# Cross attention in f32: product 7 of y ahead of product 5, T1 of e by ScalarE and transfers, in batches 2 to 5

## The chip, the cores and the metric

The kernel runs on one core of a Trainium2 chip. The metric is the device time of one execution in microseconds (us), as the median of several runs. TensorE multiplies matrices into PSUM, VectorE (DVE in the profile) and ScalarE (ACT) do the element work, GpSimd (POOL) reduces over partitions and issues the transfers that add to their destination, and SyncE (SP) issues the plain transfers. All transfers share 16 DMA engines.

## The reference

Eight batches; x1 and x2 are 512 x 1024 each, all f32. D is 64.

```
q = einsum('bcn,dc->bnd', x1, Wq) + bq
k = einsum('bcn,dc->bdn', x2, Wk) + bk[:, None]
v = einsum('bcn,dc->bdn', x2, Wv) + bv[:, None]
attn = softmax(einsum('bnd,bdm->bnm', q, k), axis=2)
out = einsum('bcm,bnm->bcn', v, attn) + x1
```

## The kernel before

The value projection is moved behind the attention: for each batch the kernel computes y = x2 times the unnormalized exponentials e (transposed), divides by the sums of e, and multiplies by Wv ("o" = Wv y). Both large products are done with seven block products instead of eight (Strassen's scheme in Winograd's form): the operands are cut into 2 x 2 blocks, and sums S1 to S4 of the left operand's blocks and T1 to T4 of the right one's are formed first. In y's first level the left blocks a["11"] to a["22"] are tiles of x2, and the right blocks are the halves of e. T1 = e12 - e11, T2 = T1 + e22, T3 = e22 + e12, T4 = e21 - T2. Most of the seven products are themselves done with seven smaller ones: left_stream (L543) forms the inner sums of a left operand, right_stream (L556) those of a right one, both as a few VectorE instructions that a caller interleaves with others (weave, L517). multiply_seeded (L764) then runs the inner steps 1, 7, 6, 2, 5, 4, 3 on TensorE. After most steps ScalarE copies the running sum ("chain", or "third") out of PSUM into the next quarter of the result, and the steps that follow add to these quarters. The function complete, returned by it, adds the copy v of step 7 to the result's second half on VectorE.

The program is one long list, written out by hand (manual schedule). Each engine runs its own instructions in the order in which the Python code issues them, and waits where an operand is not there yet or a tile's slot is still in use. A tile's slot is named by its tag; with one buffer per tag the next tile of that tag may be written only when every reader of the last one is done, transfers included.

period(s, n, nn, nnn) at L1154 is one batch's turn: s is the batch, n, nn and nnn are the next three. Batches 2 to 5 are marked s.six (L128). In such a period TensorE runs: products 1, 2 and 6 of y; the first half of n's scores (scores_0, L1180); nn's queries; products 5, 7 and 3 of y; the second half of n's scores; nn's keys; product 4 of y interleaved with product 1 of o; then products 6, 2, 5 with 7 with 3, and 4 of o.

What the change touches:

- sum_e and right_sums (L355, L394) form T1 to T4 on VectorE in two halves. In the kernel before, T1 of the next batch is formed at the end of the period (L1547), and T2 = T1 + e22 early in the next (L1272). T3 is formed in place of e12 by two adding transfers (sum_t3, L381).
- copy_t4 and add_t4 (L366, L375): T4 is -e21, copied by ScalarE, plus T2, added by two transfers of 512 KB on GpSimd's queue.
- copied_s4 and add_s4 (L150, L155): S4 likewise. evict_o (L949) brings a block of o out of PSUM; its function leave has x1 added by a transfer on GpSimd's queue (L983) and then sends the block out on SyncE's queue (L984). n.leave (L1568) is the list of leaves run in the next period.
- copy_7 (L901) takes product 7 out of bank "c" on ScalarE, negated, into tag u1; join_67 (L898) adds it to u6 on VectorE; evict_y "22" (L920) adds that to product 5 in bank "a".
- scores_0 also holds copy_u6, a transfer that adds u1 to u6 (L1185), add_t4, the running maxima of n's scores (folds), and the inner sums of product 7's right operand.
- shares (L330) inverts the sums of e and spreads them to all partitions through GpSimd's queue; lower (L338) subtracts the maximum; exponential (L347) is on ScalarE.
- project and queries (L186, L202): nn's queries use PSUM bank "c0"; load_x (L132) then fetches nn's x2 over the same tile, in four transfers on SyncE's queue.

Of the kernel before, what the change touches and what calls it, by code (L numbers as in the profile page):

```python
# [11 lines left out]
ALU = mybir.AluOpType  # L12
# [3 lines left out]
def kernel(  # L16
# [47 lines left out]
    nc = tc.nc  # L64
# [290 lines left out]
    def right_sums(t, k):  # L355

        x, y = {"T1": ("12", "11"), "T2": ("T1", "22"), "T3": ("22", "12")}[k]
        nc.vector.tensor_tensor(t[k], t[x], t[y], ALU.subtract if k == "T1" else ALU.add)
# [16 lines left out]
    def add_t4(s):  # L375

        t4 = s.t["T4"]
        for i in (0, 2):
            nc.gpsimd.dma_start(t4[:, i : i + 2, :], s.t["T2"][:, i : i + 2, :], accum_op=ALU.add)

# [172 lines left out]
    def inner_left(s, i, x, tag):  # L553
        weave(left_stream(s, i, x, tag))
# [599 lines left out]
    def period(s, n, nn, nnn):  # L1154
# [25 lines left out]
        def scores_0():  # L1180
            then = scores_and(n, 0, 1, "c", next_queries if nn else nothing)
            if s.six:
                copy_u6(s, 0)
                copy_u6(s, 1)
                nc.gpsimd.dma_start(s.tmp[6], s.tmp[1], accum_op=ALU.add)  # L1185
                add_t4(s)
                weave(folds(n, 0, "max", ALU.max), right_stream(s, 7, s.t["T3"], "yT1", "yT2"))
                highest(n, 0)
            elif s.b:
                sums_7 = right_stream(s, 7, s.t["T3"], "yT1", "yT2")  # L1190
# [77 lines left out]
        else:  # L1268
# [55 lines left out]
            if n:  # L1324
                weave(left_stream(s, 7, s.a["S3"], "yT4"))
            if s.six:
                weave(*sums_5)
            else:
                if s.b == 1:
                    sum_a(s, "S4")  # L1330
                    total_1(s)
            if n:
                if nn is None:
                    spread(s, 0)
                evict_q = scores_0()
                if nn:
                    spread(s, 0)
            if n is None:
                weave(right_stream(s, 7, s.t["T3"], "yT1", "yT2"), left_stream(s, 3, s.a["S4"], "aI3"))
# [25 lines left out]
            if n:  # L1365
                hooks |= {6: lambda: exponential(n, 0, 0), 4: lambda: exponential(n, 0, 1)}
            copy_7(s, 0)
            if n:
                lower(n, 0, 1)
# [12 lines left out]
            join_67(s)  # L1382
            evict_y(s, "22")
# [53 lines left out]
        if five:  # L1437
# [4 lines left out]
            sums_o7 = right_stream(s, "o7", s.y["T3"], "eT1")  # L1442
# [112 lines left out]
        if n:  # L1555
# [12 lines left out]
            n.leave = [last] if five else [leave, last]  # L1568
# [51 lines left out]
```

## Time and profile before

| | |
|---|---|
| median of 3 runs | 665.04 us (664.57 to 665.33) |
| profiled execution, its own time | 665.49 us |
| span from first to last instruction | 663.5 us |
| TensorE busy | 658.6 us (99%) |
| VectorE busy | 625.3 us (94%) |
| ScalarE busy | 379.0 us (57%) |
| GpSimd busy | 208.9 us (31%) |
| transferred | 129.05 MB, 195 GB/s on the mean |
| granted TensorE clock | 0.999 |

In the profile a row of a timeline gives start and length in us, the engine, the line of the kernel, the operation, what it writes and reads, and how many like it were merged; in brackets the idle time of the engine before it and what ended it. A row of a transfer group gives the issuing queue, the number, the size and the median time from issue to landing. The mean share of the 16 DMA engines in a stretch can exceed 1 a little, as packets overlap. Times in rows count from the span's start.

### The profile page before, as it was taken

The page shows a single profiled execution, that of the slowest core. Times are in us where ns is not written, and L with a number is a line of the kernel's source. Part 1 is how long each engine was busy: PE and PEld are TensorE (multiplying, and loading weights), DVE is VectorE, ACT ScalarE, POOL GpSimd, SP SyncE. Part 2 cuts the span into 40 slices and gives each one's busy share as a digit, 9 for nine tenths or more (in the row PEclk, how much of TensorE's full clock was granted, in tenths as well). Part 3 has the DMA queues.
Part 4 walks back from the last instruction along what each step waited for, and adds up shares of the span by engine and source line. Part 5 has one row for each costly group of instructions (what it writes and reads, how often), then busy time and mean ns, then how long its engine had stood idle before and what let it go on. Part 6 is the DMA issues. An engine that isn't in the chain of part 4 may idle for free.

```text
span 663.5 us, 8006 instructions
## 1 busy us (share of the span) xinstructions
PE 658.6 (99%) x2626; PEld 434.2 (65%) x2626; DVE 625.3 (94%) x890; ACT 379.0 (57%) x727; POOL 208.9 (31%) x179
## 2 busy tenths in 40 slices
PE   9999999999999999999999999999999999999997
PEld 5435755756658666677666686576865757666865
DVE  1999999999999999999999999999999999999997
ACT  3755457446475575665766646756567446474332
POOL 0125215631335402363034430354212640224300
PEclk9999999999999999999999999999999999999999
DMA  8687578994789759897598895987928995368614
GB/s 326 261 271 256 124 250 150 212 259 144 261 170 223 190 161 282 177 232 192 145 285 175 206 239 161 250 178 182 277 50 197 217 204 175 78 128 183 121 40 150
DMA packets 47368, 129.05 MB, mean 195 GB/s; under 512 B 5472, under 2 KB 5984, under 8 KB 47328
## 3 DMA queue, kind: packets, MB, share of 16 engines
q0 software_dynamic: 20336, 55.12, 45.8%
q1 hardware_dynamic: 26848, 73.29, 30.4%
q8 instruction: 21, 0.34, 0.2%
q14 instruction: 19, 0.16, 0.1%
q10 hardware_dynamic: 144, 0.14, 0.1%
HBM read 87.83 MB, written 16.81 MB: 158 GB/s over the span
## 4 chain that ended last, share of the span: by engine, by line
PE 94%; DVE 5%; issue 1%; ACT 0%
PE ps_yc L596 9%; PE ps_ya L596 7%; PE ps_oc L485 7%; PE ps_oa L730 6%; PE ps_s L236 6%; PE ps_ya L485 4%; PE ps_q L191 4%; PE ps_oa L485 4%; PE ps_i5chain L596 3%; PE ps_k L191 3%; PE ps_i7chain L596 3%; PE ps_i4b L881 3%; PE ps_i1chain L596 3%; PE ps_i2chain L596 3%; PE ps_i3chain L596 3%; PE ps_oc L881 2%
## 5 line engine op out<-in xcount | busy, mean ns | idle before, releaser
L340 DVE TENSOR_TENSOR e<-e,top 128x1024 f32<-128x1024 f32 x60 | 72.1, 1217 | 0.2 <-POOL top L272 0.2
L349 ACT ACTIVATE e<-e 128x1024 f32<-128x1024 f32 x60 | 62.8, 1058 | 15.9 <-DVE e L340 15.5
L272 POOL PARTITION_ALL_REDUCE top<-max x16 | 32.1, 2008 | 103.6 <-DVE max L266 44.2
L245 ACT COPY e<-ps_s 128x512 f32<-128x512 f32 x90 | 47.7, 619 | 10.2 <-PE ps_s L236 10.2
L304 POOL PARTITION_ALL_REDUCE den<-sum x10 | 33.4, 3337 | 43.2 <-DVE sum L266 38.3
L236 PE MATMUL ps_s<-q,k 64*128 64x512 f32 (+1 forms) x188 | 46.6, 598 | 0.0
L256 DVE TENSOR_TENSOR max<-max,e 128x1024 f32<-128x1024 f32 x30 | 36.5, 1218 | 0.3
L236 PEld LDWEIGHTS ps_s<-q,k 64*128 64x128 f32 x188 | 17.5, 186 | 19.9 <-issue 16.9
L916 DVE TENSOR_TENSOR y<-y,den 128x1024 f32<-128x1024 f32 x24 | 29.2, 1220 | 0.3
L787 ACT COPY ps_yc<-ps_i7chain 128x256 f32<-128x256 f32 x32 | 11.4, 357 | 30.2 <-PE ps_i7chain L596 25.6
L787 ACT COPY ps_ya<-ps_i1chain 128x256 f32<-128x256 f32 x28 | 10.0, 357 | 31.6 <-PE ps_i1chain L596 28.1
L730 PE MATMUL ps_oa<-yT,w_S 128*128 128x512 f32 x56 | 27.5, 592 | 0.0
L285 POOL PARTITION_ALL_REDUCE den<-sum x6 | 19.4, 3229 | 25.3 <-DVE sum L266 25.3
L730 PE MATMUL ps_oa<-y,w_S 128*128 128x512 f32 x56 | 26.3, 592 | 0.0
L325 POOL DMA_DIRECT2D den<-row x12 | 6.7, 561 | 60.0 <-DMA row<-few 36.6
L191 PE MATMUL ps_q<-x_in_x_dram,wqk_sb 128*64 128x512 f32 x112 | 25.6, 598 | 0.0
L485 PE MATMUL ps_oc<-yT,w 128*128 128x512 f32 x56 | 25.3, 594 | 0.1
L787 ACT COPY ps_ya<-ps_i5chain 128x256 f32<-128x256 f32 x32 | 11.5, 360 | 24.1 <-PE ps_i5chain L596 20.0
L485 PE MATMUL ps_oa<-yT,w_S 128*128 128x512 f32 x56 | 25.2, 593 | 0.0
L550 DVE TENSOR_TENSOR aI<-a 128x256 f32<-128x256 f32 x60 | 24.7, 411 | 0.0
L596 PE MATMUL ps_yc<-e,aI 128*128 128x256 f32 x92 | 23.6, 379 | 0.0
L983 POOL DMA_DIRECT2D r<-in_x_dram x14 | 18.3, 1309 | 15.9 <-ACT r L971 15.9
(358 smaller groups left out, 1861.3 us busy)
## 6 DMA issues: line engine op xcount, KB each, us to landing
x_in_x_dram<-in_x_dram SPq DMA_DIRECT2D x60, 512.0 KB, 7.5
a<-in_x2T_dram SPq DMA_DIRECT2D x32, 512.0 KB, 5.7
aS<-in_x2T_dram POOLq DMA_DIRECT2D x21, 512.0 KB, 5.7
eT<-eT POOLq DMA_DIRECT2D x16, 512.0 KB, 11.8
r<-in_x_dram POOLq DMA_DIRECT2D x14, 512.0 KB, 7.1
uo<-in_x_dram POOLq DMA_DIRECT2D x14, 512.0 KB, 8.8
out_dram<-r SPq DMA_DIRECT2D x14, 512.0 KB, 3.3
e<-e POOLq DMA_DIRECT2D x13, 512.0 KB, 7.1
```

The costliest lines, as they stand in the source:

```text
L191: nc.tensor.matmul(ps[r, :], w_sb[:, c, :], s.x[:, c, ts(h, H)], start=(c == 0), stop=(c == CT - 1),)
L236: nc.tensor.matmul(ps[g][:, n], s.k[r, ts(i, P)], s.q[r, ts(h, H)][:, n], start=True, stop=True)
L245: nc.scalar.copy(e[:, g, i, :], ps[g])
L256: nc.vector.tensor_tensor(f, e[:, :, 0, :] if i == 1 else f, e[:, :, i, :], op)
L304: nc.gpsimd.partition_all_reduce(s.den[h], s.mx[h][:, 0, :], P, ReduceOp.add)
L340: nc.vector.tensor_tensor(e, e, top, ALU.subtract)
L349: nc.scalar.activation(e, e, AF.Exp)
L485: nc.tensor.matmul(ps, left[ka][:, k, ts(j, P)], right[kb][:, k, :], start=opens and k == 0, stop=i in (2, 3, 4) and k == n_k - 1, skip_gr ...
L596: nc.tensor.matmul(ps, s.inner[i][ka][:, k, :], s.inner[i, "t"][kb][:, k, :], start=opens and k == 0, stop=z in (2, 3, 4) and k == n_k - 1 ...
L730: nc.tensor.matmul(ps, w[ka][:, k, ts(j, P)], s.y[kb][:, k, :], start=False, stop=i == 3 and k == 1, skip_group_check=True,)
L787: nc.scalar.copy(out, of)
L881: nc.tensor.matmul(ps, s.inner[i][ka][:, k, :], s.inner[i, "t"][kb][:, k, :], start=opens and k == 0, stop=z in (2, 3, 4) and k == n_k - 1 ...
```

## The change

In batches 2 to 5 (s.six):

- T1 of the next batch is no longer formed on VectorE. After the two transfers that form T3, ScalarE writes -e22 into T1 (begin_t1). In the next period VectorE forms T2 = T3 - e11 instead of T1 + e22, and two transfers add T2 to T1 (end_t1), so that T1 = T2 - e22.
- The leave of block 22 moves from the end of the period into n.leave, behind that of block 12; add_s4 and both leaves are issued behind end_t1.
- Product 7 runs before product 5. Its right sums are formed beside its left sums, ahead of the scores; product 5's inner sums are formed between the maxima in scores_0. add_t4 is issued first in scores_0, ahead of the addition of u1.
- nn's queries use a buffer of ps_s instead of bank c0.
- copy_7's two halves and join_67 move into and around product 5. Product 4's left sums are formed after evict_y "22" instead of after product 5.
- Tags: product 5's right sums use y21 for u1; product 3's left sums a12 for aI3 and its right sums eT2 for eT1; product 4's left sums aI3 for a12 and its right sums eT1 for eT2; product 7 of o's right sums eT2 for eT1.

```diff
@@ right_sums
-        x, y = {"T1": ("12", "11"), "T2": ("T1", "22"), "T3": ("22", "12")}[k]
-        nc.vector.tensor_tensor(t[k], t[x], t[y], ALU.subtract if k == "T1" else ALU.add)
+        x, y, op = {
+            "T1": ("12", "11", ALU.subtract),
+            "T2": ("T1", "22", ALU.add),
+            "T3": ("22", "12", ALU.add),
+            "T2 of T3": ("T3", "11", ALU.subtract),
+        }[k]
+        nc.vector.tensor_tensor(t[k[:2]], t[x], t[y], op)
...
+    def begin_t1(s):
+        for i in (0, 2):
+            nc.scalar.mul(s.t["T1"][:, i : i + 2, :], s.t["22"][:, i : i + 2, :], -1.0)
+
+    def end_t1(s):
+        for i in (0, 2):
+            nc.gpsimd.dma_start(
+                s.t["T1"][:, i : i + 2, :], s.t["T2"][:, i : i + 2, :], accum_op=ALU.add
+            )
@@ period
-            evict = queries(nn, "c0")
+            evict = queries(nn, None if s.six else "c0")
...
-        def scores_0():
+        def scores_0(*sums):
             then = scores_and(n, 0, 1, "c", next_queries if nn else nothing)
             if s.six:
+                add_t4(s)
                 copy_u6(s, 0)
                 copy_u6(s, 1)
                 nc.gpsimd.dma_start(s.tmp[6], s.tmp[1], accum_op=ALU.add)
-                add_t4(s)
-                weave(folds(n, 0, "max", ALU.max), right_stream(s, 7, s.t["T3"], "yT1", "yT2"))
+                weave(folds(n, 0, "max", ALU.max), *sums)
                 highest(n, 0)
...
-            sum_e(s, *(("T2",) if early else ("T1", "T2")))
+            sum_e(s, *(("T2 of T3",) if s.six else ("T2",) if early else ("T1", "T2")))
+            if s.six:
+                end_t1(s)
             sums_5 = (
                 left_stream(s, 5, s.a["S1"], "i2"),
-                right_stream(s, 5, s.t["T1"], "aI3" if s.six else "y21", "u1"),
+                right_stream(s, 5, s.t["T1"], "aI3", "y21") if s.six else right_stream(s, 5, s.t["T1"], "y21", "u1"),
             )
+            sums_7 = right_stream(s, 7, s.t["T3"], "yT1", "yT2")
...
+            if s.six:
+                add_s4(s)
             if n:
                 for leave in s.leave:
                     leave()
...
-            if s.b > 1:
+            if s.b > 1 and not s.six:
                 add_s4(s)
...
-            if n:
-                weave(left_stream(s, 7, s.a["S3"], "yT4"))
             if s.six:
-                weave(*sums_5)
+                weave(left_stream(s, 7, s.a["S3"], "yT4"), sums_7)
...
-                evict_q = scores_0()
+                evict_q = scores_0(*(sums_5 if s.six else (sums_7,)))
...
-            complete_5 = multiply_seeded(
-                s, 5, "r" if s.six else "top", {6: evict_q} if five and nn else {}, "a"
-            )
+            if s.six:
+                complete_7 = multiply_seeded(s, 7, "y12", {6: evict_q})
+            else:
+                complete_5 = multiply_seeded(s, 5, "top", {6: evict_q} if five and nn else {}, "a")
...
-            if s.six:
-                inner_left(s, 4, s.a["22"], "a12")
-            complete_5()
-            if s.b > 1:
+            if not s.six:
+                complete_5()
+            if s.b > 1 and not s.six:
                 shares(s, 1)
...
-                sums_3 = right_stream(s, 3, s.t["22"], "eT1")
+                sums_3 = right_stream(s, 3, s.t["22"], "eT2" if s.six else "eT1")
                 next(sums_3)
...
-                weave(*([left_stream(s, 3, s.a["S4"], "aI3")] if nn else []), sums_3)
+                weave(*([left_stream(s, 3, s.a["S4"], "a12" if s.six else "aI3")] if nn else []), sums_3)
+                if s.six:
+                    complete_7()
+                    shares(s, 1)
                 lower(n, 0, 0)
...
-            complete_7 = multiply_seeded(s, 7, "y12")
-            complete_7()
-            hooks = {7: lambda: copy_7(s, 1)}
+            hooks = {}
+            if s.six:
+                lower(n, 0, 1)
+                complete_5 = multiply_seeded(s, 5, "r", {7: lambda: copy_7(s, 0), 6: lambda: copy_7(s, 1)}, "a")
+                join_67(s)
+                complete_5()
+                evict_y(s, "22")
+            else:
+                complete_7 = multiply_seeded(s, 7, "y12")
+                complete_7()
+                hooks[7] = lambda: copy_7(s, 1)
+                copy_7(s, 0)
...
-            sums_4 = [right_stream(s, 4, s.t["T4"], "eT2")]
-            if not s.six:
-                sums_4.insert(0, left_stream(s, 4, s.a["22"], "a12"))
             if n:
-                weave(*sums_4)
+                weave(left_stream(s, 4, s.a["22"], "aI3" if s.six else "a12"), right_stream(s, 4, s.t["T4"], "eT1" if s.six else "eT2"))
...
-            sums_o7 = right_stream(s, "o7", s.y["T3"], "eT1")
+            sums_o7 = right_stream(s, "o7", s.y["T3"], "eT2" if s.six else "eT1")
...
             if nn:
-                sum_e(n, "T1")
+                if not n.six:
+                    sum_e(n, "T1")
                 sum_t3(n, 0)
                 sum_t3(n, 2)
-        if five:
+                if n.six:
+                    begin_t1(n)
+        if five and not n.six:
             leave()
...
-            n.leave = [last] if five else [leave, last]
+            n.leave = [last, leave] if n.six else [last] if five else [leave, last]
```

More of the change, by code (lines that the diff above doesn't have):

```diff
@@ L1185, in scores_0 @@
                 nc.gpsimd.dma_start(s.tmp[6], s.tmp[1], accum_op=ALU.add)
-                add_t4(s)
-                weave(folds(n, 0, "max", ALU.max), right_stream(s, 7, s.t["T3"], "yT1", "yT2"))
+                weave(folds(n, 0, "max", ALU.max), *sums)
                 highest(n, 0)
             elif s.b:
-                sums_7 = right_stream(s, 7, s.t["T3"], "yT1", "yT2")
+                sums_7, = sums
                 if nn is None:
@@ L1323, in period @@
                 first(6)
-            if n:
-                weave(left_stream(s, 7, s.a["S3"], "yT4"))
             if s.six:
-                weave(*sums_5)
+                weave(left_stream(s, 7, s.a["S3"], "yT4"), sums_7)
             else:
+                if n:
+                    weave(left_stream(s, 7, s.a["S3"], "yT4"))
                 if s.b == 1:
@@ L1338, in period @@
             if n is None:
-                weave(right_stream(s, 7, s.t["T3"], "yT1", "yT2"), left_stream(s, 3, s.a["S4"], "aI3"))
-            complete_5 = multiply_seeded(
-                s, 5, "r" if s.six else "top", {6: evict_q} if five and nn else {}, "a"
-            )
+                weave(sums_7, left_stream(s, 3, s.a["S4"], "aI3"))
+            if s.six:
+                complete_7 = multiply_seeded(s, 7, "y12", {6: evict_q})
+            else:
+                complete_5 = multiply_seeded(s, 5, "top", {6: evict_q} if five and nn else {}, "a")
             if n and nn is None:
                 weave(left_stream(s, 3, s.a["S4"], "aI3"))
-            if s.six:
-                inner_left(s, 4, s.a["22"], "a12")
-            complete_5()
-            if s.b > 1:
+            if not s.six:
+                complete_5()
+            if s.b > 1 and not s.six:
                 shares(s, 1)
@@ L1361, in period @@
                 inner_right(s, 3, s.t["22"], "eT1")
-            complete_7 = multiply_seeded(s, 7, "y12")
-            complete_7()
-            hooks = {7: lambda: copy_7(s, 1)}
+            hooks = {}
[10 more added lines that the diff above has]
+                copy_7(s, 0)
             if n:
                 hooks |= {6: lambda: exponential(n, 0, 0), 4: lambda: exponential(n, 0, 1)}
-            copy_7(s, 0)
-            if n:
+            if n and not s.six:
                 lower(n, 0, 1)
@@ L1381, in period @@
                 lower(n, 0, 2)
-            join_67(s)
-            evict_y(s, "22")
+            else:
+                join_67(s)
+                evict_y(s, "22")
             if n is None:
                 weave(right_4)
-            sums_4 = [right_stream(s, 4, s.t["T4"], "eT2")]
-            if not s.six:
-                sums_4.insert(0, left_stream(s, 4, s.a["22"], "a12"))
             if n:
-                weave(*sums_4)
+                weave(left_stream(s, 4, s.a["22"], "aI3" if s.six else "a12"), right_stream(s, 4, s.t["T4"], "eT1" if s.six else "eT2"))
             complete_3()
```

## The prediction

> **What bounds the kernel now.** I read the busy totals first, then who TensorE waited for, then the busy time of each batch period, then the stretches inside one period, then single rows of that period. In short: TensorE is full, so the question is where the change can make it wait.
>
> The totals, and all waits of TensorE that its view of waits lists:
>
> ```profile
> PE 658.6 (99%) x2626; PEld 434.2 (65%) x2626; DVE 625.3 (94%) x890; ACT 379.0 (57%) x727; POOL 208.9 (31%) x179
> q0 software_dynamic: 20336, 55.12, 45.8%
> q1 hardware_dynamic: 26848, 73.29, 30.4%
> PE ps_warm L1070 <- DVE warm L1067: 1.0, 1, 1.0
> PE ps_oc L485 <- DVE y L916: 0.2, 1, 0.2
> ```
>
> Busy time by periods (from one block of scores of the second half to the next; two of the four that change, the next one, and the tail), then by products of batch 3's period. After the colon: length, then PE, PEld, DVE, ACT, POOL busy, granted clock, DMA share, GB/s.
>
> ```profile
> 240.37:320.71 80.34, 80.34 (x330) 55.09 (x330) 77.54 (x112) 49.55 (x97) 27.77 (x25) 1.00 0.83 206
> 401.06:481.40 80.34, 80.34 (x330) 55.10 (x330) 77.30 (x112) 49.55 (x97) 27.75 (x25) 1.00 0.82 207
> 481.40:561.75 80.35, 80.35 (x312) 52.83 (x314) 75.60 (x107) 48.16 (x93) 26.33 (x22) 1.00 0.73 174
> 561.75:663.50 101.75, 97.92 (x364) 67.43 (x360) 96.00 (x144) 45.81 (x96) 23.22 (x19) 1.00 0.50 114
> 276.87:282.92 6.05, 6.05 (x30) 5.32 (x29) 5.98 (x11) 2.11 (x6) 2.39 (x3) 1.00 1.07 204
> 282.92:288.96 6.04, 6.04 (x30) 5.32 (x28) 6.04 (x9) 3.27 (x8) 5.42 (x4) 1.00 1.06 218
> 288.96:295.00 6.04, 6.04 (x29) 5.12 (x27) 5.97 (x12) 3.27 (x8) 2.52 (x1) 1.00 1.05 250
> 295.00:302.30 7.30, 7.30 (x33) 2.60 (x32) 7.27 (x14) 5.94 (x12) 2.63 (x5) 1.00 0.47 122
> 302.30:308.46 6.16, 6.16 (x30) 5.42 (x29) 6.13 (x10) 3.08 (x7) 3.95 (x5) 1.00 0.91 198
> ```
>
> The reader is to see three things. In the periods that change, TensorE is busy for the whole period (80.34 of 80.34) at full clock: there is no wait to remove. VectorE has 77.3 to 77.5, so about 3 us free. The DMA engines, full from 276.87 to 295.00, have room only at 295.00 to 302.30 (0.47, some 3.9 us unused). All that can be won lies in the tail, where 101.75 - 97.92 = 3.8 us are unfilled, and those belong to batches that the change does not touch.
>
> **The change, part by part** (times in batch 3's period; the batch there is "s").
>
> *T1 of e leaves VectorE.* Two instructions, 2.35 us, go; ScalarE gets two of the size of its row L177, 1.05 us each, and has room before product 1:
>
> ```profile
> 272.39 2.35 DVE L358 TENSOR_TENSOR eT<-e,e 128x1024 f32<-128x1024 f32 x2
> 271.95 1.05 ACT L177 ACTIVATE aS<-aS 128x1024 f32<-128x1024 f32 x1
> 277.99 0.36 ACT L787 COPY ps_ya<-ps_i1chain 128x256 f32<-128x256 f32 x1 [2.72 <-PE ps_i1chain L596]
> 284.12 2.72 DVE L358 TENSOR_TENSOR eT<-eT,e 128x1024 f32<-128x1024 f32 x2
> ```
>
> 2.1 us fit into 2.72 of idle time: no cost on ScalarE; without that cover, 2.1 us before product 1's first eviction. The gain on VectorE is worth nothing by itself, since it waits for product 1 anyway, and the new T2 = T3 - e11 waits for T3's transfers, which landed at 284.1 (next fence). So T2 ends where it did, near 286.8.
>
> *Two more transfers of 512 KB, in a ring that is already the fullest thing here.* POOL's transfers land in order; five issues in a row, with the landing time of the first and the last:
>
> ```profile
> 273.29 0.88 POOL L181 DMA_DIRECT2D aS<-in_x2T_dram  x1 [7.37 <-ACT aS L177]
> 274.17 0.88 POOL L384 DMA_DIRECT2D e<-e  x1
> 275.67 0.88 POOL L384 DMA_DIRECT2D e<-e  x1 [0.62 <-DVE eI1yT L573]
> 276.21 1.58 POOL L983 DMA_DIRECT2D uo<-in_x_dram  x1
> 276.92 1.81 POOL L181 DMA_DIRECT2D a<-in_x2T_dram  x1
> aS<-in_x2T_dram POOLq DMA_DIRECT2D x1, 512.0 KB, 5.3
> e<-e POOLq DMA_DIRECT2D x1, 512.0 KB, 8.5
> a<-in_x2T_dram POOLq DMA_DIRECT2D x1, 512.0 KB, 12.2
> ```
>
> First 273.29 + 5.3 = 278.6, T3's second half 275.67 + 8.5 = 284.1 (its wait is for T1's reading, and goes), last 276.92 + 12.2 = 289.1: four more transfers in 10.5 us, 2.63 each. A plain transfer of SP's costs 0.304 x 663.5 / 73.29 MB x 0.524 MB = 1.44 us of all engines.
>
> After the change block 22's addition is not in front of S3's, so S3 lands at 289.1 - 2.6 = 286.5. Then come T1 (two), S4, block 12, block 22: 5 x 2.63 = 13.2, with two output transfers of SP between them (block 21, block 12), 2.9. Block 22's addition lands at 302.5; T1 itself lands at about 293, in time for its readers, which now stand between the maxima that end at 306.4. T4's two transfers, though issued earlier (near 297, not 302), start only then.
>
> *Why T4's landing now matters.* Product 3's right sums move from tile eT1 into eT2, which holds T2, and T4's transfers read T2. VectorE is in order: with the first of these sums (r3) wait product 3's left sums (l3), product 7's completion, the shares and two subtractions. In the old order that slot held product 4's left sums, which waited for nothing. How fast the ring moves while the next batch's x comes in is seen here (the second row is the second of the first row's two):
>
> ```profile
> 301.60 0.92 POOL L1185 DMA_DIRECT2D uy<-uy  x1 [4.37 <-ACT ps_i5third L782]
> 302.77 1.53 POOL L379 DMA_DIRECT2D eT<-eT  x1
> eT<-eT POOLq DMA_DIRECT2D x1, 512.0 KB, 15.0
> ```
>
> The last lands at 317.8. Of 317.8 - 301.6 = 16.2 us, 2.7 are issue and latency (5.3 - 2.63), so 3 x 2.63 = 7.9 us took 13.5: the ring keeps 0.58 of its pace beside the loads of x. T4's two then take 5.26 / 0.58 = 9.1 us and land at **311.6**. Without any slowing they would land at 307.8; at half pace at 313.0.
>
> *When VectorE must start.* The new product 5 stands where 7 stood. Its last step begins at 313.64 and needs ScalarE's copy of step 5, behind copy_7's second half, behind product 7's completion, behind r3 and l3:
>
> ```profile
> 305.73 0.68 DVE L266 TENSOR_TENSOR max<-max 128x512 f32<-128x512 f32 x1
> 309.20 1.19 DVE L578 TENSOR_TENSOR eI3eT<-e 128x1024 f32<-128x1024 f32 x1
> 312.85 1.22 DVE L340 TENSOR_TENSOR e<-e,top 128x1024 f32<-128x1024 f32 x1
> 314.23 0.70 DVE L804 TENSOR_TENSOR ps_yc<-ps_yc,v 128x512 f32<-128x512 f32 x1 [0.16 <-ACT ps_yc L787]
> 313.64 1.03 PE L596 MATMUL ps_yc<-e,aI 128*128 128x256 f32 x4
> 312.98 0.36 ACT L787 COPY ps_yc<-ps_i7chain 128x256 f32<-128x256 f32 x1 [1.37 <-PE ps_i7chain L596]
> 316.70 0.60 ACT L904 ACTIVATE uy<-ps_yc 128x512 f32<-128x512 f32 x1
> ```
>
> r3 and l3 take 312.85 - 309.20 = 3.65; completion 0.70, copy_7 0.60, the copy 0.36: 5.31 in all. So r3 must start by 313.64 - 5.31 = 308.3 (308.4 with the handing on and the 0.17 below). VectorE is free for it from 306.4. It starts at 311.6: TensorE stands still for **3.2 us** in product 5.
>
> What is late next is covered. join_67 needs the addition of u1, now behind T4, at 311.6 + 2.63 / 0.58 = 316.1; VectorE gets there at 311.6 + 3.65 + 0.70 + 0.2 + 2.4 = 318.5. The x loads are needed by the keys' projection, behind product 3 and a block of scores, and the stall moves that back too.
>
> *Queries in a ps_s buffer.* They take the buffer of the third scores, first half, whose copy is the first of these four:
>
> ```profile
> 298.22 2.10 ACT L245 COPY e<-ps_s 128x512 f32<-128x512 f32 x4
> 298.73 3.65 PE L191 MATMUL ps_q<-x_in_x_dram,wqk_sb 128*64 128x512 f32 x16
> ```
>
> 2.10 for four that overlap: the first ends near 298.85, and the next instruction gets there some 0.05 later, against 298.73: **0.17 us**, between 0 and 0.6 (one more copy).
>
> The other moves (a12 and aI3 exchanged, eT1 and eT2 in o7, y21 for u1, the leaves behind S4) cost nothing: product 2 has long read a12, the output's buffers are next written after 302, and products 6 and 4 have freed the rest.
>
> *Sum:* 4 periods x (3.2 + 0.17) = 13.5 us on the profiled execution's 665.49 (span 663.5 and 2.0 around it): 679.0. The median of the runs, 665.04, is 0.45 lower: **678.5**. Ends: no stall, 665.0 + 0.7 = 665.7; half pace, T4 at 313.0, 4.6 + 0.17 each, 684.1.
>
> The Trainium skill, "DMA: Bandwidth & Descriptors", section "Queues, rings and completion order", says that each engine goes round the queue rows that have work, packet by packet. Equal turns would give the ring half its pace, T4 at 313.0 and some 684; the row above says 0.58, and I keep the row.
>
> **The rivals.**
>
> A, *not slower*: T4 lands by 308.4. For it: only 3.2 us lie between, the unslowed landing is 307.8, and the engines have 3.9 us unused before 302. Against: 5.3 us of new transfers must fit there, and x arrives in the same microseconds. Then only the queries' 0.17 x 4 remain: 665.7. A landing just after the deadline gives each microsecond late back four times over.
>
> B, *the stall closes the clock*. At the start of the program TensorE ran its first 16 query matmuls in 5.00 us, where 16 of these later take 3.58:
>
> ```profile
> 4.39 5.00 PE ps_q L1029 x16
> 31.37 3.58 PE ps_q L191 x16
> ```
>
> If 3 us of standing still brings that back, 1.4 us more each time: 678.5 + 5.7 = 684.2. For it: the same engine, cold. Against: before the change no stall in the middle is long enough to show it. The Trainium skill, "TensorE: Matmul & The Clock Gate", section "Part 1: The HAM clock gate (the "warmup" mystery)", puts the idle window at about 3.4 us, so it might just be missed; no trace here tells.
>
> C, *the lag runs on*. VectorE is some 1 us later against TensorE after product 3; it has about that much to wait in product 4. If not, product 6 of o waits a further microsecond: 678.5 + 4 = 682.5.
>
> D, *faster*: the freed VectorE time reaches the tail and takes over a third of its 3.8 us. Against: TensorE is full up to 561.75, and the tail's batches keep their code. 663.5.
>
> **How the numbers follow.** Forecast 0.60, A 0.14, B 0.12, C 0.12, D 0.02. Runs of this kernel lie within 664.57 to 665.33, so 0.2% (1.3 us) is about what can be told from no change. Faster 0.02 (D), same 0.13 (A but for a sliver), slower 0.85. The range leaves out A, D and what lies beyond half pace with a cold clock: 668 to 688.
>
> **What would show it.** Right: T4's transfers (line of add_t4) land after 309, r3's first sum has idle time before it that ends with that landing, and TensorE idles some 3 us in the last step of product 5, four times, with periods near 83.7 us. Wrong: r3 starts at 306 to 308; or periods of 80.3; or the idle time stands elsewhere (before queries, at product 4), or the granted clock falls below 1.00 in the middle.

## The result, and the profile after

The changed kernel takes 667.83 us (median of 7 runs, 666.48 to 668.73), the kernel before in the same comparison 665.72 us (7 runs, 664.57 to 666.26). The ratio is 1.003, 95% interval 1.0017 to 1.0043. It is slower by 2.1 us; the forecast was 13.5 us more, with a range from 668 up. The profiled execution of the changed kernel took 667.40 us, its span is 665.5.

The totals of the changed kernel's page, its two large queues, and TensorE's waits (us in total, times, longest):

```profile
PE 659.4 (99%) x2626; PEld 435.0 (65%) x2626; DVE 610.7 (92%) x882; ACT 385.7 (58%) x735; POOL 216.1 (32%) x187
q0 software_dynamic: 21488, 59.32, 48.6%
q1 hardware_dynamic: 26848, 73.29, 30.5%
...
PE ps_warm L1087 <- DVE warm L1084: 1.0, 1, 1.0
PE ps_k L449 <- DMA x_in_x_dram<-in_x_dram: 0.8, 2, 0.5
PE ps_oc L502 <- DVE y L933: 0.2, 1, 0.2
```

VectorE lost 14.6 us of work, ScalarE took 6.7 more, GpSimd's queue carries 4.2 MB more. The four stalls of 3.2 us in product 5 are not in the list. The one new entry is a wait of the keys for x, in a place that the change does not touch.

Three of the four changed periods, in the columns of the prediction's windows:

```profile
240.37:320.71 80.34, 80.25 (x328) 54.92 (x327) 73.01 (x109) 50.94 (x98) 29.27 (x26) 1.00 0.89 218
320.71:401.06 80.35, 80.25 (x329) 55.06 (x328) 74.36 (x111) 51.28 (x98) 29.68 (x27) 1.00 0.89 220
401.06:481.40 80.34, 80.24 (x329) 55.07 (x328) 72.57 (x108) 51.26 (x98) 28.78 (x26) 1.00 0.89 220
```

VectorE fell from 77.5 to about 73 us in a period, the DMA engines rose from 0.83 to 0.89, and TensorE stands for 0.1 us instead of 0.

Where the 2 us arose is found by laying the start of the same TensorE instruction in the two traces side by side. The lag at a marker is its time in the changed kernel less its time in the kernel before:

| marker in the changed kernel's trace | us | lag, us |
|---|---|---|
| queries of batch 2 (head of the program) | 57.36 | 1.13 |
| keys ahead of the first changed period | 164.70 | 1.11 |
| queries, keys of the first changed period | 219.66, 245.40 | 1.28, 1.47 |
| of the second | 300.36, 325.97 | 1.63, 1.69 |
| of the third | 380.93, 406.48 | 1.86, 1.86 |
| of the fourth | 461.44, 486.99 | 2.03, 2.03 |
| last matmul | 661.68 | 2.02 |

So 1.1 us were lost before any changed code ran, 0.17 us just ahead of each of the four batches of queries (0.68), and 0.25 between queries and keys, where products 7, 5 and 3 stand. Nothing came back.

### The profile page after: what moved, and what is told of

It is laid out like the page before. It is cut to its first block, busy times and chain, and to the rows that moved or that the text cites. A ratio compares the mean times of both kernels' runs of the same rounds, so it can differ in the third digit from the quotient of the medians.

```text
span 665.5 us, 8055 instructions
## 1 busy us (share of the span) xinstructions
PE 659.4 (99%) x2626; PEld 435.0 (65%) x2626; DVE 610.7 (92%) x882; ACT 385.7 (58%) x735; POOL 216.1 (32%) x187
## 4 chain that ended last, share of the span: by engine, by line
PE 90%; DVE 5%; ACT 2%; DMA 1%; issue 1%; SPq 0%
PE ps_yc L613 9%; PE ps_ya L613 7%; PE ps_oc L502 7%; PE ps_oa L747 6%; PE ps_s L236 5%; PE ps_ya L502 4%; PE ps_q L191 4%; PE ps_oa L502 4%; PE ps_i5chain L613 3%; PE ps_i7chain L613 3%; PE ps_k L191 3%; PE ps_i4b L898 3%; PE ps_i3chain L613 3%; PE ps_i1chain L613 3%; PE ps_i2chain L613 3%; PE ps_oc L898 2%
## 5 line engine op out<-in xcount | busy, mean ns | idle before, releaser
L349 ACT ACTIVATE e<-e 128x1024 f32<-128x1024 f32 x60 | 62.8, 1057 | 15.7 <-DVE e L340 15.4
L1000 POOL DMA_DIRECT2D r<-in_x_dram x14 | 20.3, 1453 | 14.9 <-ACT r L988 14.9
L285 POOL PARTITION_ALL_REDUCE den<-sum x6 | 19.4, 3230 | 17.8 <-DVE sum L266 17.8
L256 DVE TENSOR_TENSOR max<-e 128x1024 f32<-128x1024 f32 x15 | 20.4, 1357 | 5.0 <-ACT e L245 5.0
```

The costliest lines, as they stand in the source:

```text
L256: nc.vector.tensor_tensor(f, e[:, :, 0, :] if i == 1 else f, e[:, :, i, :], op)
L349: nc.scalar.activation(e, e, AF.Exp)
```

## Was the mechanism there?

The period to compare with the prediction is the second (batch 3). It comes with a lag of 1.47 us, which has to be taken off; the 0.17 us that its own queries add is already in the prediction's limit of 308.4. GpSimd's issues in it (T1's two, S4, block 12, block 22, T4's two, u1), with times from issue to landing, then the first right sum of product 3 on VectorE, and ScalarE's copy of product 5's step 7:

```profile
286.47 0.88 POOL L394 DMA_DIRECT2D eT<-eT  x1 [0.80 <-PE ps_i2third L613]
287.54 0.87 POOL L394 DMA_DIRECT2D eT<-eT  x1 [0.19 <-issue]
288.08 1.21 POOL L160 DMA_DIRECT2D aS<-in_x2T_dram  x1
288.62 1.91 POOL L1000 DMA_DIRECT2D r<-in_x_dram  x1
289.33 2.41 POOL L1000 DMA_DIRECT2D uo<-in_x_dram  x1
297.62 1.87 POOL L384 DMA_DIRECT2D eT<-eT  x2
303.05 0.85 POOL L1203 DMA_DIRECT2D uy<-uy  x1 [3.56 <-ACT uy L406]
uo<-in_x_dram POOLq DMA_DIRECT2D x1, 512.0 KB, 14.2
...
309.84 1.23 DVE L595 TENSOR_TENSOR eI3eT<-e 128x1024 f32<-128x1024 f32 x1 [2.15 <-DMA eT<-eT]
...
312.30 0.37 ACT L804 COPY v<-ps_i5third 128x256 f32<-128x256 f32 x1 [0.73 <-DMA out_dram<-r]
```

Block 22's addition landed at 289.33 + 14.2 = 303.5; less the lag that is 302.0, the forecast was 302.5. T4's two landed at 306.09 and 309.40 in the trace's record of landings: 304.6 and 307.9 on the clock of the prediction, which had the second at 311.6. VectorE's first right sum waits for just that landing (2.15 us idle, ended by eT<-eT), as forecast. But it starts in time: on the prediction's clock at 309.84 - 1.47 = 308.4, just at the limit of 308.4, and TensorE is not held by it. The queries start at 298.73 in the kernel before, 298.90 with their own wait; counted from there, as times of a period are below, the limit is 308.4 - 298.9 = 9.5 us, and this sum started at 309.84 - 300.36 = 9.48.

The shares of the DMA engines that each queue had in three stretches of the same period tell why T4 came sooner (packets, MB, share of 16 engines; packets overlap, so that a sum may exceed 100%). In order: 301:304, 304:306, and 306.1:309.4 (T4's second transfer):

```profile
q0 software_dynamic: 296, 0.64, 112.6%
out_dram<-r SPq DMA_DIRECT2D x1, 512.0 KB, 11.2
...
q0 software_dynamic: 110, 0.39, 97.3%
q1 hardware_dynamic: 27, 0.06, 8.2%
...
q0 software_dynamic: 117, 0.41, 62.8%
q1 hardware_dynamic: 263, 0.52, 43.1%
```

In the first stretch SyncE had already issued block 12's output (at 301.00) and its queue has no row at all: not one packet was served. The first one came 4.4 us after the issue, where in e4_t4late (below) it came 0.9 us after. In the second stretch the queue got 8%. Only beside T4's second transfer are the shares near the 0.58 that the prediction used for both, and near those that the kernel before had in the stretch from which that 0.58 came (304:311):

```profile
q0 software_dynamic: 180, 0.67, 60.6%
q1 hardware_dynamic: 315, 1.16, 42.2%
```

So the first went at full pace, 306.09 - 303.5 = 2.6 us, and the second took 3.3, 5.9 together where 9.1 were forecast. The price was paid by the plain transfers: block 12's output took 11.2 us. That output is read out of the tile with tag r, and it is its landing that ends the last row above, the wait of ScalarE's copy v. This wait is not in the prediction.

The Trainium skill, "DMA: Bandwidth & Descriptors", section "Queues, rings and completion order", has an engine go round the queue rows with work packet by packet. The trace does not agree with equal turns here: 112.6% against nothing, then 97.3 against 8.2, then 62.8 against 43.1. Whether the engines passed over packets that were ready, or the plain queue's packets were late, the trace does not tell.

## The experiments

The first profile can be read in two ways. By the first, the stall that was forecast exists and T4's landing only fell on the good side of the limit: later landings cost one for one, and what is lost beside the queries is lost where T4 is late. By the second, the new order is not sensitive to T4, and the 2 us are the queries and the chance of the head. Each ratio below is to the kernel before, run beside it on the same chip (665.65 to 665.86 us), with its 95% interval. The lags are those of the profiled execution, against the trace of before, and need no median:

| kernel | ratio | lag ahead of the 4 periods | added at the 4 queries | added between queries and keys, 4 periods | lag at the end |
|---|---|---|---|---|---|
| changed, first profile | 1.003 | 1.11 | 0.68 | 0.19, 0.06, 0, 0 | 2.02 |
| a0_after | 1.0028 | -0.29 | 0.68 | 1.81, 0.10, 0, 0 | 2.30 |
| a1_after | 1.0024 | 0.82 | 0.68 | 0.18, 0.02, 0, 0 | 1.69 |
| b0_before | 0.9998 | 0 | 0 | 0 | 0 |
| e1_bank2 | 1.0016 | 1.13 | 0 | 1.18, 0.69, 0, 0 | 3.00 |
| e2_before_psq | 1.0013 | 1.00 | 0.70 | 0 | 1.70 |
| e3_r3late | 1.002 | 2.01 | 0.66 | 0.98, 0.41, 0, 0 | 4.06 |
| e4_t4late | 1.0704 | 1.06 | 0.67 | 9.74, 10.63, 12.37, 11.04 | 45.50 |
| e5_t1dve | 1.0017 | 0.06 | 0.70 | 0 | 0.76 |
| e7_y12 | 0.9999 | 1.69 | 0 | 0 | 1.69 |
| e8_leave12 | 1.0053 | -0.71 | 0.66 | 1.08, 1.27, 0.28, 0.48 | 3.06 |

**The changed kernel again (a0_after).** No edit; the question is how far one execution stands for the others.

> The changed kernel once more. Its first profile is 2.0 us longer than that of before: 1.13 at the keys of batch 1 (period 0, which the change does not touch), 4 x 0.17 ahead of the queries, 0.25 behind late transfers of T4. Theory 1 (spread): the 1.13 is a chance of that execution, this profile has another amount there or none, and the timed median lies 0.9 to 1.5 us above before. Theory 2 (the program as a whole): the same 1.1 us stand there again, and the median lies 2 us above before.

Measured: 667.69 us (9 runs, 666.61 to 669.1), 1.0028 [1.0018, 1.0038]. Neither theory holds alone: the head's loss is gone from the profile, as the first said, but the median lies 1.83 us over before, above its 0.9 to 1.5. The profile has other places of loss than the first: nothing at the head, but 1.81 us in product 5 of the first changed period and what follows it. TensorE's waits, then VectorE's first right sum, ScalarE's copy v, and the two TensorE steps that stood still:

```profile
PE ps_i5chain L613 <- ACT ps_ya L804: 0.9, 1, 0.9
PE ps_ya L613 <- ACT ps_ya L804: 0.2, 1, 0.2
...
229.36 1.23 DVE L595 TENSOR_TENSOR eI3eT<-e 128x1024 f32<-128x1024 f32 x1 [3.76 <-DMA eT<-eT]
...
231.33 0.37 ACT L804 COPY v<-ps_i5third 128x256 f32<-128x256 f32 x1 [1.86 <-DMA out_dram<-r]
...
232.53 1.13 PE L613 MATMUL ps_i5chain<-eI5aI,aI 128*128 128x256 f32 x4 [0.92 <-ACT ps_ya L804]
234.70 1.13 PE L613 MATMUL ps_ya<-eT,aI 128*128 128x256 f32 x4 [0.18 <-ACT ps_ya L804]
```

There are two waits, one after the other. The first sits two steps ahead of the last one: ScalarE's copy v waited 1.86 us for out_dram<-r, the copies behind it came late, and TensorE needed them. Undisturbed, v starts 11.66 us after the period's queries in every trace of the new order; here 13.07, 0.10 after the output landed (12.97). The second is the one that was forecast: T4 landed 11.01 us after the queries, the sum started at 11.10 where the limit is 9.5, and the last step stood once more, by less, since the first wait had already moved it. Product 3 starts 17.41 us after the queries instead of 15.78: 1.63 late, against 11.10 - 9.5 = 1.6.

**Queries in the next buffer of ps_s (e1_bank2).** In scores_0 the third block of scores instead of the second goes to bank c, so that the ps_s buffer of the queries is not the one whose copy has just begun.

```diff
-            then = scores_and(n, 0, 1, "c", next_queries if nn else nothing)
+            then = scores_and(n, 0, 2 if s.six else 1, "c", next_queries if nn else nothing)
```

> The changed kernel with n's third scores instead of the second in bank c, so that the queries take a PSUM buffer that was copied two copies earlier. Theory 1: the 0.17 us ahead of the queries is gone in all four periods, 0.7 us less than the changed kernel in the same call, all else equal. Rival: TensorE then waits 0.2 us elsewhere (the fourth scores for the first's copy), no gain.

Measured: 666.57 us, 1.0016 [1.0006, 1.0025]; that is 1.12 us under a0_after, with intervals that overlap. The lag no longer grows at any of the four queries. Product 5 lost more in this execution, again behind the copy v: the output landed 12.77 and 12.47 us after the queries, v started at 12.87 and 12.57, and the step that stood is the earlier one.

```profile
PE ps_i5chain L613 <- ACT ps_ya L804: 1.1, 2, 0.7
```

T4 landed at 10.21 and 9.51, and the right sums started at 10.31 and 9.96: behind the limit too, but by less than what the copy had taken. So the queries' wait is real and separable, and it is not all.

**The queries alone, in the kernel before (e2_before_psq).**

```diff
-            evict = queries(nn, "c0")
+            evict = queries(nn, None if s.six else "c0")
```

> The kernel before with one edit: queries in a ps_s buffer in batches 2 to 5. Theory 1: 0.17 us ahead of the queries in each of four periods, 0.7 us over before, nothing else. Theory 2 (the 2 us need the transfers): also 0.7, but then the remaining 1.3 us of the change must show with the transfers alone. If it gives 0, the queries' wait is taken up elsewhere.

Measured: 666.5 us, 1.0013 [1.0004, 1.0021]; 0.18, 0.17, 0.18 and 0.17 us at the four queries, nothing in product 5. Its profile also has a whole microsecond of lag ahead of the periods, where the only wait is this one, with code that is that of the kernel before:

```profile
PE ps_k L432 <- DMA x_in_x_dram<-in_x_dram: 0.9, 1, 0.9
```

The head's wait for x is therefore not a part of the change: the changed kernel has it (first profile, a1_after) and lacks it (a0_after), and so do kernels with the old order. Whether the change makes it more frequent is not settled.

**Product 3's right sums last (e3_r3late).** The completion of product 7 and the shares no longer stand behind the sum that waits for T4.

```diff
-                next(sums_3)
+                if s.six:
+                    inner_left(s, 3, s.a["S4"], "a12")
+                    complete_7()
+                    shares(s, 1)
+                else:
+                    next(sums_3)
                 if s.b == 1:
                     shares(s, 1)
-                weave(*([left_stream(s, 3, s.a["S4"], "a12" if s.six else "aI3")] if nn else []), sums_3)
-                if s.six:
-                    complete_7()
-                    shares(s, 1)
+                weave(*([left_stream(s, 3, s.a["S4"], "aI3")] if nn and not s.six else []), sums_3)
```

> The changed kernel with product 7's completion and the shares issued ahead of product 3's right sums on VectorE, behind its left sums, so that no completion stands behind the wait for T4's transfers. Theory 1 (late T4 costs in the timed executions, where it may land later than in the profile): the 0.25 us in products 5 and 3 go, and the median falls by 0.3 to 1 us against the changed kernel, with a smaller spread. Theory 2 (T4 costs nothing beyond the profile's 0.25): falls by 0.25 at most, spread as before.

Measured: 666.87 us, 1.002 [1.001, 1.0031]. The median is 0.82 us under a0_after, as the first theory had it, but the intervals overlap and the spread (665.90 to 669.46) is no smaller: not to be told from the changed kernel. In its profile 0.98 and 0.41 us were still lost with T4 taken out of the way:

```profile
PE ps_k L449 <- DMA x_in_x_dram<-in_x_dram: 1.4, 2, 0.8
PE ps_i5chain L613 <- ACT ps_ya L804: 0.5, 1, 0.5
```

This goes against the first reading in its pure form: product 5 waits for something else as well. ScalarE's copy v stood at 12.68 and 12.29 us after the queries, the output's landing at 12.58 and 12.19. The output that holds tag r became a third theory. Its limit comes out of e1_bank2's and this kernel's four periods: product 3 starts late by 1.00, 0.69, 0.80 and 0.42 us where v starts at 12.87, 12.57, 12.68 and 12.29, so the limit for v is 11.88 us each time, to 0.01.

**T4's transfers behind u1 again (e4_t4late).** One line moves, to where the kernel before had it; the landing comes 8 to 11 us later.

```diff
             if s.six:
-                add_t4(s)
                 copy_u6(s, 0)
                 copy_u6(s, 1)
                 nc.gpsimd.dma_start(s.tmp[6], s.tmp[1], accum_op=ALU.add)
+                add_t4(s)
```

> The changed kernel with T4's transfers issued behind u1's addition again, as in the kernel before. Theory 1 (the chain of the prediction holds, only the landing was placed too late): T4's second transfer lands 13 to 19 us after the queries begin instead of 9; product 5 stalls by its landing less 9.5 us, 4 to 9 us in each of four periods, and the time is 680 to 705. Theory 2 (the wait behind T4 does not reach TensorE): below 670.

Measured: 711.63 us (4 runs), 1.0704 [1.0678, 1.0729], above the 680 to 705 that were expected. The wait is exactly the forecast one, in product 5's last step, four times:

```profile
PE ps_ya L613 <- ACT ps_ya L804: 33.6, 4, 9.9
...
236.90 1.23 DVE L595 TENSOR_TENSOR eI3eT<-e 128x1024 f32<-128x1024 f32 x1 [9.95 <-DMA eT<-eT]
...
242.23 2.07 PE L613 MATMUL ps_ya<-eT,aI 128*128 128x256 f32 x4 [7.55 <-ACT ps_ya L804]
```

T4 landed 17.27, 17.11, 19.55 and 17.99 us after the four queries, 71.92 together; less four times the limit of 9.5 that makes 33.9, and 33.6 were measured. Limit and slope of the prediction hold. The four matmuls of the last row take 2.07 us instead of 1.03, and the windows of that stretch (231:239, 239:245.8, 245.8:255) show the granted clock, the figure behind the last busy time:

```profile
231.00:239.00 8.00, 3.68 (x18) 2.90 (x16) 2.10 (x4) 1.23 (x3) 0.00 (x0) 1.00 1.01 272
239.00:245.80 6.80, 3.57 (x8) 2.86 (x9) 6.80 (x12) 1.14 (x3) 1.11 (x2) 0.50 0.58 211
245.80:255.00 9.20, 9.20 (x43) 5.88 (x43) 9.17 (x16) 6.33 (x13) 0.00 (x0) 1.00 0.08 23
```

The clock fell while TensorE still stood. The stall began at 242.23 - 7.55 = 234.68, and the clock is 0.50 from 239 to 245.8: from 4.3 us into the stall to 3.6 us behind its end. In the other three periods it fell 2.8, 3.8 and 3.1 us into the stall and stayed at 0.50 for 10.2 us. The four periods lost 43.8 us by the table, 10.2 more than the stalls. TensorE worked for 17.8 us at the slower clock, and half of that, 8.9 us, is its price. Nearly all the rest comes from the view of waits, which shows 0.27 us less for each stall than the lag grows (1.00 for 1.27 in e8_leave12 below). The plain output was quick here, with only block 22's addition left in the ring: SyncE issued out_dram<-r at 220.78, and it took 3.8 us.

```profile
out_dram<-r SPq DMA_DIRECT2D x1, 512.0 KB, 3.8
```

**T1 on VectorE again (e5_t1dve).** T1's two transfers and ScalarE's two instructions go; the order of the products stays.

```diff
-            sum_e(s, *(("T2 of T3",) if s.six else ("T2",) if early else ("T1", "T2")))
-            if s.six:
-                end_t1(s)
+            sum_e(s, *(("T2",) if early else ("T1", "T2")))
...
-                if not n.six:
-                    sum_e(n, "T1")
+                sum_e(n, "T1")
...
-                if n.six:
-                    begin_t1(n)
```

> The changed kernel with T1 formed on VectorE again, so without the two added transfers a period; all else as changed. Theory 1 (the ring's load makes block 12 leave late, and with it product 5's copy of step 7): block 12 has left well before 11.6 us after the queries' start, no stall in product 5, 0.17 x 4 remain: 0.7 over before. Theory 2 (the order of products costs by itself): as the changed kernel, 1.8 over before.

Measured: 666.79 us, 1.0017 [1.0008, 1.0025]. T4 lands 7.94, 8.06 and 7.21 us after the first three queries, the output by 1.44, and product 5 has no wait at all. The lag is the queries' 0.70 and nothing else. VectorE is busy for 76.6 us of a period instead of 73:

```profile
240.37:320.71 80.34, 80.23 (x329) 55.08 (x328) 76.58 (x113) 49.31 (x97) 27.61 (x24) 1.00 0.85 206
```

3.6 us more of VectorE's time in this period cost nothing, and in this execution product 5 lost nothing without the two transfers. The profile is as the first theory had it; the median is 1.1 us over before instead of 0.7, and by medians alone e5_t1dve is not to be told from the changed kernel.

**All three waits taken away (e7_y12).** The edits of e1_bank2 and e3_r3late, and product 5's copy v in tag y12, so that it does not wait for block 12's output.

```diff
-                complete_5 = multiply_seeded(s, 5, "r", {7: lambda: copy_7(s, 0), 6: lambda: copy_7(s, 1)}, "a")
+                complete_5 = multiply_seeded(s, 5, "y12", {7: lambda: copy_7(s, 0), 6: lambda: copy_7(s, 1)}, "a")
```

> The changed kernel with three edits: third scores in bank c, product 7's completion ahead of product 3's right sums, product 5's copy of step 7 in tag y12 instead of r, so that it does not wait for block 12 to leave. Theory 1 (these three waits are all of it): TensorE has no wait in the four periods, and the time is that of before, within 0.3 us. Theory 2 (something else in the added transfers costs): still 0.5 us or more over before, with waits at another place.

Measured: 665.45 us, 0.9999 [0.9988, 1.001]: the time of the kernel before. In its profile the output lands 13.16, 12.22 and 11.34 us after the first three queries and T4 as late as 11.29, and still v starts at 11.66 each time and TensorE waits nowhere in the four periods; the 1.69 us of lag are the head's (this execution took 667.23 us):

```profile
PE ps_k L449 <- DMA x_in_x_dram<-in_x_dram: 1.1, 2, 0.8
PE ps_warm L1087 <- DVE warm L1084: 1.0, 1, 1.0
PE ps_oc L502 <- DVE y L933: 0.2, 1, 0.2
```

**The kernel before beside itself (b0_before).** No edit.

> The kernel before itself, for a further profile. Theory 1: the stall at the keys of batch 1 (1.13 us in the first profile of the changed kernel, 0.74 in that of before with the queries moved) is a chance of the execution, between 0 and 1.7 us, and can show here too. Theory 2 (it belongs to changed programs): none here.

Measured: 665.53 us, 0.9998 [0.9988, 1.0007]. The keys of batch 1 have no wait; the queries of batch 2 come 0.24 us earlier than in the first profile of the same kernel, and no marker behind them has a lag.

**Block 12's leave ahead of T1's transfers (e8_leave12).** Tried as the simplest cure of the tag's wait.

```diff
             if s.six:
+                s.leave.pop(0)()
                 end_t1(s)
```

> The changed kernel with one edit: block 12's leave is issued ahead of T1's two transfers instead of behind them and S4. Theory 1: block 12 has left before product 5's copy of step 7 in all four periods, that copy never waits, the stalls at step 5 of product 5 go; T4 lands where it did, so those at its last step and in product 3 stay. 0.4 to 1.2 us less than the changed kernel in the same call. Theory 2 (the two waits share one cause, the ring's length): no gain, since the ring moves as many bytes.

Measured: 669.07 us (5 runs, 668.44 to 670.19), 1.0053 [1.004, 1.0066], 1.84 us over a1_after, which ran beside it, where 0.4 to 1.2 us less were expected: a miss, the slowest but e4_t4late. The output lands by 2.5 to 4.0 us after the queries and v is always at 11.66, as meant. But T4 now lands at 10.27, 10.29, 9.65 and 9.85, all behind the limit, and product 3 starts late in all four periods, by 0.90, 1.27, 0.28 and 0.48 us. Three of these waits are long enough for the list. Its row, then the second period:

```profile
PE ps_ya L613 <- ACT ps_ya L804: 1.8, 3, 1.0
...
310.17 1.23 DVE L595 TENSOR_TENSOR eI3eT<-e 128x1024 f32<-128x1024 f32 x1 [3.40 <-DMA eT<-eT]
...
315.51 1.13 PE L613 MATMUL ps_ya<-eT,aI 128*128 128x256 f32 x4 [1.00 <-ACT ps_ya L804]
```

In this period the sum started 10.74 us after the queries (310.17 - 299.43), 1.24 behind the limit, and the lag grew by 1.27. The ring has the same work ahead of T4 as in the changed kernel, but the output's bytes, which there moved beside and behind T4's second transfer, now go ahead of it. So the plain transfer's delay had helped T4 to land in time. The output itself was no quicker: it took 9.6 to 10.7 us from issue to landing.

**The changed kernel a third time (a1_after),** beside e8_leave12.

> The changed kernel a third time, beside the last one. Both theories: 1.8 to 2.1 us over before. Theory 1: this profile has again other amounts at the keys of batch 1 and in product 5, and each stall at step 5 of product 5 has block 12 landing later than 11.6 us after the queries' start.

Measured: 667.23 us, 1.0024 [1.0015, 1.0033], 1.58 us over before and so a little under the 1.8 to 2.1 expected; 0.20 us between queries and keys in its profile, 0.82 ahead of the periods, again with the keys' wait:

```profile
PE ps_k L449 <- DMA x_in_x_dram<-in_x_dram: 1.2, 1, 1.2
```

**What follows of the theories.** That T4's landing sets product 5's last step, one for one behind a limit, is shown (e4_t4late, e8_leave12). That the new order does not feel T4 is wrong: in the three profiles of the changed kernel it set three of the four late starts of product 3 (1.63 and 0.10 us in a0_after, 0.03 in a1_after). But it is not all: the copy v set the fourth (0.06 us in the first profile), would have cost 1.19 of the 1.63 by itself, and set all of e1_bank2's and e3_r3late's. The output that holds tag r is the second edge, and with all three waits gone the loss is gone (e7_y12). Product 3 starts late by the larger of two amounts, the first right sum's start less 9.47 and v's start less 11.88, to 0.02 us in all 24 changed periods of the first profile, a0_after, a1_after, e1_bank2, e5_t1dve and e8_leave12. In the changed kernel's 1.6 to 2.1 us of the medians, the queries are 0.7 in every profile; product 5 and what follows had 0.2 to 1.9 us in three profiles.

Two things stay open. The first changed period adds 0.19 us more behind the start of product 3, in each kernel but e5_t1dve and e7_y12 (and e2_before_psq, which has the old order). It arises at one place, in product 3: ScalarE's first copy out of its chain starts 1.40 us behind the product's start instead of 1.12 (e4_t4late apart, where the clock is slow). No experiment was made on it. And how the rest of the medians is shared between product 5 and the head cannot be told from three profiles. e7_y12 has the same head, and its median is that of before, with an interval of -0.8 to 0.7 us; that speaks for product 5, without showing it.

## Why the prediction was wrong, point by point

- **The term that failed: T4's landing.** "T4's two then take 5.26 / 0.58 = 9.1 us and land at 311.6." They took 5.9 and landed at 307.9. The pace of 0.58 had been read off three transfers that ran beside loads of x, from a ring that had been empty; it was applied to two that stood behind a filled ring. While that ring was full the plain queue got nothing, then 8%. Why it did is not shown by any run. The forecast stall of 3.2 us came in no period of the first profile, where r3 started at most 0.01 us behind the limit; in one period of a0_after it was 1.6 us. Of the 13.5 us forecast, 4 x 3.2 = 12.8 hung on this term alone.
- **Block 22's landing** (302.5; measured 302.0) and with it the 2.63 us for each added transfer: right.
- **The limit of 308.4 and its slope:** right. r3 had to start 9.5 us after the queries; e8_leave12's second period puts the limit at 10.74 - 1.27 = 9.47, and e4_t4late's four stalls sum to 33.6 where the rule gives 33.9.
- **The queries' 0.17 us, four times:** right to 0.01 in all eight traces that have the queries' edit as it is, and gone in the two in which the queries have another buffer.
- **VectorE's time is worth nothing by itself:** right. 3 to 5 us less work in each period moved no marker, and e5_t1dve, which gives most of it back, lost nothing in product 5. ScalarE's 2.1 us are hidden: no lag arose in products 1, 2 and 6.
- **"The other moves ... cost nothing":** wrong in one of them. "The output's buffers are next written after 302" is true, 310.8 on the prediction's clock, but block 12's output reads tag r until it lands, and this landing had been moved too: the leave stands behind T1 and S4, and its plain transfer behind the whole ring. It landed at 299.5 before and, on the same clock, at 310.7 after. The prediction watched when the tag is written and not when it comes free.
- **The rivals.** A, not slower, was given 0.14 and 665.7 us; its condition, T4 by 308.4, was met in the first profile, and it came nearest. It lacks the tag's wait, and T4's own in those executions in which it lands late. B, a closed clock, did not happen, since stalls up to 1.2 us (the longest, a1_after's at the head) left the granted clock at 1.00. In e4_t4late it fell to 0.50, and it fell 2.8, 3.1, 3.8 and 4.3 us into the four stalls. So the mechanism exists, and a stall of the forecast 3.2 us could have met its condition or missed it; no run had one. The Trainium skill, "TensorE: Matmul & The Clock Gate", section "Part 1: The HAM clock gate (the "warmup" mystery)", has the idle window at about 3.4 us; the four times lie on both sides of that. C, a lag that runs on, and D, a faster tail, left no trace: from the last changed period to the end the lag is constant to 0.01 us.
- **The range** began at 668 and left A out; the measured 667.83 lies between A's price and the range. That the kernel came out slower was forecast, and in part for the right reasons: the queries' 0.7 us is in every profile, T4's wait in two of three, with 1.73 and 0.03 us. But the stall of 3.2 us in every period did not come and tag r's wait was not foreseen, so the direction is in part luck. The bounds of the ring's pace were taken from 0.5 to 0.58, though "without any slowing they would land at 307.8" stood in the working. The landing was bounded only on the slow side, 0.6 us from the limit on the other.

## What to carry to other kernels

Where one engine is full at full clock, as here, freeing another buys nothing; what is left are the waits that the edit brings in by moving transfers and buffers, a loss that at best slack hides. A landing has to be bounded at both paces of its queue, and where the limit lies between the two, no central value is worth much. For every tile that a moved instruction writes, look up who holds its slot last, transfers included, and where that holder's transfer now stands in its queue.

## What the runs showed of the hardware that was not expected

- Plain transfers beside a filled queue of adding transfers were not slowed by a share but at first held back: block 12's output had no packet for 4.4 us after its issue, then its queue had 8.2% of the engines, then 43.1%. It took 11.2 us. In e4_t4late, where T4 wasn't ahead of it, the first packet came after 0.9 us and the whole took 3.8.
- Issuing that plain transfer of 512 KB some 7 us sooner made the adding transfers behind it 0.6 to 1.3 us later (e8_leave12: T4 at 10.27, 10.29, 9.65, 9.85 us after the queries; first profile of the changed kernel: 9.09, 9.04, 8.38, 9.22) and the kernel slower. The output was held back there as well, with its first packet 3.6 to 3.8 us after the issue.
- In e4_t4late the granted clock fell to 0.50 after 2.8 to 4.3 us of standing and stayed there for 6.8 us once and 10.2 us three times; 17.8 us of TensorE's work ran at that clock, which cost some 8.9 us on top of 33.6 of stalls. At the end of the twelve profiles it fell 2.5 to 5.4 us behind the last matmul.
- The head of the program has a wait for x that comes and goes between executions of one and the same program. At the queries of batch 2 the three profiles of the changed kernel lie 1.13, -0.27 and 0.84 us from the kernel before, with no change made yet there: a spread of 1.4 us, two thirds of the whole effect.
